# Two projections in tiles of their own, a bias by a product, statistics joined on GpSimd, and three moves in the order of work

## The chip, the cores and the metric

The kernel runs on one core of a Trainium2 chip. A core has a matrix engine (TensorE, called PE in the profile; its weight loads are listed apart as PEld), VectorE (DVE), ScalarE (ACT), GpSimd (POOL) and SyncE (SP), which here only issues DMAs. Each engine runs its own instruction stream in order, and engines wait for one another by semaphores. SP and ACT each have a hardware DMA queue. The metric is the device time of one execution in microseconds, the median of several runs.

## The reference

Input are x and ctx, both (8, 256, 256) in fp32. Two layers are computed, each an attention and a mixture of experts.

1. *Autocorrelation attention.* q = x Wq + bq and k = ctx Wq + bq (256 to 16 columns, the same bias), v = ctx Wq + bq. The circular correlation of q and k over the sequence is averaged over batch and channel, the 12 largest of its 256 lags are taken, and their softmax weighs shifted copies of v. The 16 heads are alike. The result goes through Wout and is added to x.
2. *Balanced assignment.* Scores are layernorm(x) times 8 centroids. Expert 0 takes the 256 tokens with the highest score, expert 1 the best 256 of the rest, and so on. Each expert is 256 to 1024, gelu, 1024 to 256.
3. *Cross attention* of the result with ctx (keys and values from Wkv, 16 heads).
4. *Top-2 mixture of experts* with gated experts and shared ones.

Core of the first two:

```python
q = (Q @ Wq + bq).transpose(0, 2, 1)
k_ = (K @ Wq + bq).transpose(0, 2, 1)
corr = real(ifft(fft(q) * conj(fft(k_)))).mean(axis=(0, 1))
...
for e in range(E):
    s = where(taken, -inf, scores[:, e])
    _, idx = top_k(s, C)
    taken = taken.at[idx].set(True)
```

## The kernel before

The order of the work is written out by hand: the order in which the program names instructions is their order on each engine. PSUM tiles come from pools: `ps_k` with 2 banks, `ps_t` with 4 (tag "pt"), `ps_a` with one bank each for "pqk" and "pg". The program orders all accesses of different engines to one PSUM tile, reads as well as writes.

*Loads (L1296 to L1337).* X and C (the two inputs, in quarters of 512 KB, tiles X and C) and the weights go out on SP's and ACT's queues. Each DMA of these two queues signals one of eight completion counters, given out in turn, and a DMA whose counter is in use waits until the earlier DMA of that counter has landed. The bias bq is needed 8 times over, down the partitions. It goes to DRAM (bqd, L1309) in 8 copies and comes back as a column (bqc, L1320).

*Attention (L1512 to L1790).* PE turns X and C quarter by quarter (`turn`, into XT and CT), while DVE and GpSimd make layernorm's statistics of X. `project` multiplies with Wq: q into half 0 and k into half 1 of the tile pqk (L1445). Rq (row factors of q) is copied out on ACT. ACT then reads k with its bias (L1594) and DVE multiplies q by Rq (L1596). PE makes the Gram product pg (L1674), whose diagonals are summed through a skewed round trip in DRAM (Gd, L1686 and L1694). DVE picks the top lags (L1755 to L1785) and writes them to Wd, and the circulant weights CW come back from there (L1781). In CW's wait PE makes small products into the tile pw: three columns of centroid products, copied by DVE to WCn (L1878), and the search's bounds (pb, L1877), from which DVE makes the steps and offsets of the search (`step`, `off`). Then comes the product with CW (pr, L1906), which DVE scales into R (L1915).

*Rows and statistics (L1918 to L2096).* PE puts x and the attention together, batch by batch ("po"). `take` makes layernorm's statistics of a batch on DVE (two bn_stats and bn_aggr pairs, `tile_stats` L1461 and L1462), copies it out on ACT and stores it to NMd, the table of tokens in DRAM. `act_sums` (L1977 to L1999) does a batch on ACT and GpSimd. `factors` makes the reciprocal standard deviation: eps added (L1471), a power on GpSimd (L1472), one Newton step (L1475 to L1478) in `newton`, and the mean factors (L1481, L1482) in `means`. `widen` (L2013, L2015) and `factor_rows` (L1950) turn factors into rows in one PSUM tile psr; `factors_out` (L2027) copies a half to srow, and `times_factors` (L2024) multiplies the raw scores: n0 for expert 0, SC for the rest. `store_factors` (L1930) puts the factors into NMd, next to their tokens. `attention_columns` (L1360 to L1391) makes, in steps, the norms of the key columns for a bound on the later softmax (`qmax`).

*Searches (L2135 to L2460).* SC goes to SCd in DRAM and row e of it is loaded across all partitions (`load_row`, L2135; SP's queue). `search` (L2158) finds for each expert the threshold that leaves 256 tokens, in rounds: DVE counts (above, L2166), PE sums the counts (pcn, L2183), DVE chooses. `list_tokens` (L2221 to L2291) makes the list of tokens (ob, pid, ids) and gathers them from NMd (R). `ffn` runs the expert on PE (ph L2372, py L2389), DVE adds the bias b2b (Y, L2398), and the rows are scattered to Yd. Each expert's weights are loaded by `load_l0` (L1807, L1809), for experts 0 and 1 ahead of the rows (L1816); the bias b2b is loaded where its expert begins (L2330). All of these are issued by SP, whose DMAs of one queue are worked off by 16 DMA engines, each in its own order.

While PE would wait in this part it works on pieces of the keys and values of the cross attention, 0.43 us each, that lie ready in a list (`work`); `fill(us)` takes as many as the given time holds. FILLS (L2446) sets for each search how much goes ahead of the first count's product, and in each round. After the last expert's search PE is the only limit to the end of the kernel.

Of the kernel before, what the change touches and what calls it, by code (L numbers as in the profile page):

```python
# [19 lines left out]
P = 128  # L20
# [1066 lines left out]
def fast_path(  # L1087
# [195 lines left out]
    bcol = pk.tile([P, 2, NB], F32, name="bcol")  # L1283
    bqd = dram.tile([1, P], F32, name="bqd")
    bkd = dram.tile([1, D], F32, name="bkd")
# [11 lines left out]
    for dst, src, i in (  # L1297
# [9 lines left out]
        nc.sync.dma_start(out=dst[:, i : i + 4, :], in_=src[:, i : i + 4, :])  # L1307

    nc.scalar.dma_start(  # L1309
        out=bqd.rearrange("o (b c) -> (o b) c", b=B),  # L1310
        in_=L0_xattn_bq.partition_broadcast(B),
    )
    nc.scalar.dma_start(
# [5 lines left out]
    nc.scalar.dma_start(out=cen[:, 2, :], in_=L0_ffn_ln_b.partition_broadcast(E))  # L1319
    nc.scalar.dma_start(out=bqc, in_=bqd.rearrange("o (p x) -> p (o x)", x=1))  # L1320
    for src, dst in (
# [34 lines left out]
    bqm = pk.tile([P, NB, 2], F32, name="bqm")  # L1356
    qmax = pk.tile([P, NB], F32, name="qmax")
    kmax = pk.tile([P, NB, NTB], F32, name="kmax")

# [3 lines left out]
    def attention_columns():  # L1363


        for c in range(NB):
            nc.vector.tensor_scalar(
                bqm[:, c, :], mask, bcol[:, 0, c : c + 1], None, ALU.mult
            )
        babs = small.tile([P, NB], F32, tag="babs", name="babs")  # L1370
        nc.vector.scalar_tensor_tensor(
            babs, bcol[:, 0, :], -1.0, bcol[:, 0, :], ALU.mult, ALU.max
        )
        yield

        pn = ps_t.tile([P, NB], F32, tag="pt", name="pn")
        for c in range(NB):
            for kc in range(KC):
                nc.tensor.matmul(
                    pn[:, c : c + 1],  # L1380
                    wsq[:, kc, c * P : (c + 1) * P],
                    ones[:, 0:1],
                    start=(kc == 0),
                    stop=(kc == KC - 1),
                )
            yield
        nc.scalar.activation(qmax, pn, AF.Copy, scale=257.0)
        nc.gpsimd.tensor_tensor(
            qmax, qmax, powers[:, 1:2].to_broadcast([P, NB]), ALU.pow
        )  # L1390
        nc.gpsimd.tensor_tensor(qmax, qmax, babs, ALU.add)  # L1391
        yield

# [42 lines left out]

    pqk = ps_a.tile([P, 2, S], F32, tag="pqk", name="pqk")

    def project(which, weights, src):

        for kc in range(KC):
            for m in range(2):
                for g in range(4):
                    b = 2 * g + m
                    nc.tensor.matmul(  # L1445
                        pqk[32 * g : 32 * g + 32, which, :],
                        weights[:, kc, DH * (1 - m) : DH * (3 - m)],
                        src[:, kc, b * S : (b + 1) * S],
                        start=(m == 0 and kc == 0),
                        stop=(m == 1 and kc == KC - 1),  # L1450
                        skip_group_check=True,
                    )
            yield
# [40 lines left out]
    bsel = pr.tile([P, NCT, 16], F32, name="bsel")  # L1494
    nc.vector.tensor_copy(bsel, fold.to_broadcast([P, NCT, 16]))
    nc.gpsimd.memset(VA[:, :, :, DH:], 0.0)
    nc.gpsimd.memset(VA[:, :, :, DH : DH + 1], 1.0)
# [37 lines left out]
    turn(X, XT, 0, act, act)  # L1535
    turn(C, CT, 0, act, dve)
    pwm = ps_a.tile([P, 3 * DH], F32, tag="pg", name="pwm")
    for kc in range(KC):
# [4 lines left out]
    for kc in range(KC):  # L1543
        nc.vector.memset(WC[:, kc, 0:DH], 0.0)
        nc.vector.memset(WC[:, kc, 2 * DH :], 0.0)
    newton()
    newton = stats_x(4, nc.gpsimd)
# [18 lines left out]
    )  # L1566
    list(project(0, WC, XT))
    turn(C, CT, 12, act, act)
# [10 lines left out]
    nc.vector.memset(cenP, 0.0)  # L1579
    projected = project(1, WZ, CT)  # L1580
    next(projected)
# [11 lines left out]
    list(projected)  # L1593
    nc.scalar.activation(qk[:, 1, :], pqk[:, 1, :], AF.Identity, bias=bqc)  # L1594

    nc.vector.tensor_tensor(qk[:, 0, :], pqk[:, 0, :], Rq, ALU.mult)  # L1596
    nc.gpsimd.tensor_copy(WK, wkv[:, :, :, 0, :])
# [126 lines left out]
    for kc in range(KC):  # L1724
        for g in range(4):
# [7 lines left out]
            )  # L1733
    columns = attention_columns()
    next(columns)
    pb1 = ps_t.tile([P, E * NF], F32, tag="pt", name="pb1")
# [78 lines left out]
    Od = dram.tile([T + P, D], F32, name="Od")  # L1815
    W0 = {e: load_l0(e) for e in range(2)}  # L1816

# [37 lines left out]
    WCn = pa.tile([P, 3, 32], F32, name="WCn")  # L1855
    pw = ps_t.tile([P, 4, 32], F32, tag="pt", name="pw")
    pb = pw[:, 3, 0:E]
# [18 lines left out]
    small_products(2)  # L1876
    nc.tensor.matmul(pb, ones[:E, :], bdiag, start=True, stop=True)  # L1877
    nc.vector.tensor_copy(WCn, pw[:, 0:3, :])  # L1878
    bound = pr.tile([P, E], F32, name="bound")
# [78 lines left out]

    def take(bs):

        for b in bs:
            for h in range(TPB):
                q = TPB * order_b.index(b) + h
                tile_stats(MV[:, q, :], pos[b][:, h, :])
            nc.scalar.copy(rows_of(b), pos[b])
# [60 lines left out]
    def factors_out(m):  # L2026
        nc.scalar.copy(srow[:, m, :], psrs[0][:, m].rearrange("p h t -> p (h t)"))  # L2027
# [5 lines left out]
    squares = act_sums(b[3])  # L2033
    take(b[:1])
    squares()
    take(b[1:2])
    pcp = ps_t.tile([P, 32], F32, tag="pt", name="pcp")
# [6 lines left out]
    spread_rows(*b[6:])  # L2044
    take(b[2:3])
    cP = pa.tile([P, 32], F32, name="cP")
    nc.vector.tensor_tensor(cP, pcp, WCn[:, 2, :], ALU.add)
    newton_a, means_a = factors(0, 8, nc.gpsimd)
    newton_a()

# [17 lines left out]
    take(b[4:6])  # L2068
    next(columns)
    widen(0, 8, nc.scalar)  # L2070
    newton_2, means_2 = factors(8, 12, nc.gpsimd)
    factor_rows(0)
    factor_rows(1)
    rows_part(psx, cP)
    next(columns)
    take(b[6:])
    newton_3, means_3 = factors(12, 16, nc.vector)
    factors_out(0)
    newton_2(nc.vector)
    widen(8, 12, nc.scalar)  # L2080
    factor_rows(2)
    means_a()
    store_factors(0)
    times_factors(n0, ps0, 0)
    newton_3()
    widen(12, 16, nc.vector)
    factor_rows(3)
    times_factors(SC, psx, 0)
    means_2()
    means_3(nc.gpsimd)  # L2090
    store_factors(1)
    factors_out(1)
    nc.scalar.copy(sx1, psx[:, halves[1]])
    times_factors(n0, ps0, 1)
    nc.gpsimd.tensor_tensor(SC[:, halves[1]], sx1, srow[:, 1, :], ALU.mult)
    next(columns)  # L2096

# [44 lines left out]

    nc.sync.dma_start(out=SCd, in_=SC)
    rows = {e: load_row(e) for e in range(1, 3)}
    nc.sync.dma_start(
# [3 lines left out]
    nc.sync.dma_start(out=Od[T:, :], in_=blank[:, 0:D])  # L2149
    rows.update({e: load_row(e) for e in range(3, E - 1)})  # L2150

    def search(e, row, steps, head, each):
# [292 lines left out]

    FILLS = {0: (0.43, [1.29] * 4), 1: (2.15, [1.29] * 4)}  # L2446
    FILLS[2] = FILLS[3] = (2.15, [1.73, 2.58, 1.73, 1.73])
# [1006 lines left out]
```

## Time and profile before

| | us |
|---|---|
| median of 3 runs | 877.67 (877.28 to 878.70) |
| the profiled execution | 878.58 |
| its span | 876.9 |
| PE busy | 854.9 (98%) |
| DVE, ACT, POOL busy | 306.5, 266.1, 213.3 |

Some moments of the profiled execution, in us from the span's start:

| | start |
|---|---|
| first turn of C's third quarter (C8) | 15.99 |
| k from ACT, then q from DVE | 22.94, 23.44 |
| Gram product pg | 23.93 |
| small products out (WCn), R | 39.38, 41.47 |
| last factor rows | 55.57 |
| first count of search 0, first step of search 1 | 57.11, 71.45 |
| Y of the first expert | 95.70 |

A line of the timeline gives the start, the duration, the engine, the line of the kernel, the operation, the output and its inputs, the shapes, and in brackets how long the engine had been idle and who released it. A line of the waits gives the engine and what it was about to do, whom it waited for, and the sum, the number and the longest of such waits. Matmuls are pipelined and their ends are modelled. The profile's span is 1.7 us shorter than the time of the same execution.

### The profile page before, as it was taken

To read this page: it belongs to the slowest core of one execution; us is meant where nothing else is said; L and a number is where in the kernel's file an instruction comes from. 1 tells how busy PE (TensorE), PEld (TensorE's weight loads), DVE (VectorE), ACT (ScalarE), POOL (GpSimd) and SP (SyncE) were. 2 spreads that over 40 slices of the span, in tenths; PEclk is the share of its full clock that TensorE was granted. 3 is DMA by queue.
4 is the path that set the end of the run, shared out by engine and by line. 5 is a ranking of instruction groups with operands and counts; after the bars stand their busy time and mean duration, and the time that the engine had idled before them with its cause. 6 is when DMAs were issued, how large, how long until landed. Compare 5 with 4: busy or idle time off the path is not lost.

```text
span 876.9 us, 11139 instructions
## 1 busy us (share of the span) xinstructions
PE 854.9 (98%) x4178; PEld 533.2 (61%) x4178; DVE 306.5 (35%) x1022; ACT 266.1 (30%) x494; POOL 213.3 (24%) x293
## 2 busy tenths in 40 slices
PE   8999999999999999999999999999999999999997
PEld 7546788788455555545568474747474657474745
DVE  5377876412656765551111212020111111111021
ACT  4344443332677675321110111111111111111110
POOL 7261222302235464423310020201111131111200
PEclk9999999999999999999999999999999999999999
DMA  8385479831610001361111545555657434311130
GB/s 248 132 231 180 158 204 274 277 125 39 167 36 26 1 20 38 122 227 44 68 50 40 177 142 148 163 174 156 181 156 181 150 92 114 85 13 12 18 103 28
DMA packets 87254, 105.22 MB, mean 120 GB/s; under 512 B 8952, under 2 KB 77784, under 8 KB 87160
## 3 DMA queue, kind: packets, MB, share of 16 engines
q1 hardware_dynamic: 78520, 91.10, 33.1%
q0 software_dynamic: 7920, 13.02, 7.1%
q8 instruction: 35, 0.57, 0.3%
q10 hardware_dynamic: 752, 0.30, 0.1%
q14 instruction: 27, 0.22, 0.1%
HBM read 80.61 MB, written 25.37 MB: 121 GB/s over the span
## 4 chain that ended last, share of the span: by engine, by line
PE 87%; DMA 5%; DVE 3%; POOL 2%; ACT 1%; issue 1%; SPq 0%; POOLq 0%; DVEq 0%; ACTq 0%
PE pgt L3074 19%; PE py L3096 19%; PE pu L3074 19%; PE py L2389 5%; PE ph L2372 4%; PE p L2651 4%; PE pv L2666 3%; DMA R<-NMd,ids 3%; PE pp L2717 2%; PE pp L2618 2%; PE pp L1419 2%; PE pp L1398 1%; PE pgu L3269 1%; PE pt L3130 1%; PE pt L1512 1%
## 5 line engine op out<-in xcount | busy, mean ns | idle before, releaser
L3083 DVE TENSOR_TENSOR A<-A,pu 128x512 f32<-128x512 f32 x96 | 66.1, 688 | 364.9 <-PE pu L3074 358.4
L3082 ACT ACTIVATE A<-pgt 128x512 f32<-128x512 f32 x96 | 57.4, 598 | 271.4 <-PE pgt L3074 271.4
L3143 POOL DMA_INDIRECT Od<-Y,ids x32 | 49.7, 1552 | 304.0 <-ACT Y L3156 206.7
L3074 PE MATMUL pgt<-RT,wa 128*128 128x512 f32 x256 | 121.1, 595 | 0.0
L3074 PE MATMUL pu<-RT,wb 128*128 128x512 f32 x256 | 120.3, 592 | 0.0
L3096 PE MATMUL py<-wc,A 128*128 128x256 f32 x512 | 111.8, 379 | 0.0
L3096 PEld LDWEIGHTS py<-wc,A 128*128 128x128 f32 x512 | 96.7, 190 | 13.3 <-issue 0.5
L3074 PEld LDWEIGHTS pu<-RT,wb 128*128 128x128 f32 x256 | 48.6, 190 | 61.2 <-issue 60.0
L2659 ACT ACTIVATE ex<-p,scale 128x512 f32<-128x512 f32 x128 | 77.3, 690 | 27.5 <-PE p L2651 26.2
L3074 PEld LDWEIGHTS pgt<-RT,wa 128*128 128x128 f32 x256 | 47.6, 190 | 54.9 <-issue 54.5
L2372 PE MATMUL ph<-RT,w 128*128 128x256 f32 x256 | 61.7, 389 | 0.8 <-ACT RT L2359 0.7
L2389 PE MATMUL py<-w,A 128*128 128x256 f32 x256 | 61.6, 388 | 0.0
L2372 PEld LDWEIGHTS ph<-RT,w 128*128 128x128 f32 x256 | 45.3, 190 | 8.9 <-ACT A L2381 1.1
L2389 PEld LDWEIGHTS py<-w,A 128*128 128x128 f32 x256 | 46.6, 190 | 6.4
L2891 POOL DMA_INDIRECT Td<-HP,to x32 | 31.7, 991 | 64.5 <-DMA Td<-HP,to 63.8
L2381 ACT ACTIVATE A<-ph,b1c 128x256 f32<-128x256 f32 x64 | 30.1, 473 | 53.9 <-PE ph L2372 49.6
L3074 PE MATMUL pgt<-HT,wa_-1_2734 128*128 128x512 f32 x96 | 45.5, 596 | 0.0
L3074 PE MATMUL pu<-HT,wb_-1_2735 128*128 128x512 f32 x96 | 45.1, 592 | 0.0
L3156 ACT ACTIVATE Y<-py,R 128x256 f32<-128x256 f32 x32 | 15.2, 474 | 96.5 <-PE py L3096 96.5
L2651 PE MATMUL p<-QM,KT 32*128 32x512 f32 x256 | 43.4, 640 | 0.4 <-DVE QM L2632 0.4
L3096 PE MATMUL py<-wc_-1_2736,A 128*128 128x256 f32 x192 | 41.9, 379 | 0.0
L3096 PEld LDWEIGHTS py<-wc_-1_2736,A 128*128 128x128 f32 x192 | 36.4, 190 | 5.8 <-issue 1.0
(445 smaller groups left out, 982.2 us busy)
## 6 DMA issues: line engine op xcount, KB each, us to landing
w<-in_L_ffn_w_dram SPq DMA_DIRECT2D x16, 1024.0 KB
wa<-in_L_ffn_w_e_dram SPq DMA_DIRECT2D x8, 1024.0 KB
wb<-in_L_ffn_w_e_dram SPq DMA_DIRECT2D x8, 1024.0 KB
wc<-in_L_ffn_w_e_dram SPq DMA_DIRECT2D x8, 1024.0 KB
R<-Td SPq DMA_DIRECT2D x8, 530.0 KB
sa<-in_L_ffn_w_e_dram SPq DMA_DIRECT2D x16, 256.0 KB
sb<-in_L_ffn_w_e_dram SPq DMA_DIRECT2D x16, 256.0 KB
sc<-in_L_ffn_w_e_dram SPq DMA_DIRECT2D x16, 256.0 KB
```

The lines of the kernel that those rows point to most:

```text
L2372: nc.tensor.matmul(ph, w1[:, kc, f * P : (f + 1) * P], RT[:, kc, :], start=(kc == 0), stop=(kc == KC - 1),)
L2381: nc.scalar.activation(A[:, f, :], ph, AF.Gelu_apprx_tanh, bias=b1c[:, e, f : f + 1])
L2389: nc.tensor.matmul(py, A[:, f, r * P : (r + 1) * P], w2[:, f, :], start=(f == 0), stop=(f == NF - 1),)
L2651: nc.tensor.matmul(ps[g].rearrange("p m q -> p (m q)"), KT[rows, c, k0 : k0 + P], QM[b][rows, c].rearrange("p m q -> p (m q)"), start=True ...
L2659: nc.scalar.activation(e4[:, g], ps[g], AF.Exp, scale=scale)
L2666: nc.tensor.matmul(pvs[b, c][32 * g : 32 * g + 32, m, :], VA[:, b * TPB + kt, 8 * c + 2 * g + m, :], ex[b, c, kt][:, g, m, :], start=(kt = ...
L2891: nc.gpsimd.indirect_dma_start(out=Td, out_offset=bass.IndirectOffsetOnAxis(ap=to[g][:, k, j : j + 1], axis=0), in_=HP[:, GT * g + j, :], ...
L3074: nc.tensor.matmul(ps, w_[:, kc, fs], xs[kc], start=(kc == 0), stop=(kc == KC - 1),)
L3082: nc.scalar.activation(a, pgt, AF.Silu)
L3083: nc.vector.tensor_tensor(a, a, pu, ALU.mult)
L3096: nc.tensor.matmul(py, A[:, f, s : s + P], wc[:, f, :], start=(f == 0), stop=(f == NF - 1))
L3143: nc.gpsimd.indirect_dma_start(out=Od, out_offset=bass.IndirectOffsetOnAxis(ap=ids, axis=0), in_=Y, in_offset=None, compute_op=ALU.add,)
```

## The change

1. The bias bq is loaded as one column of 16 (`bq16`); both DMAs of the round trip through DRAM go. GpSimd copies a repeated unit matrix (`rep16`), a small product `pbq` spreads the bias over the partitions, and DVE copies it to bqc.
2. q and k get a PSUM tile each: `pq` where pqk was, and `pk_` from the pool of the turned tiles.
3. The products of the column norms leave the stretch of rows and statistics and go into a fifth column block of pw, after pb and ahead of the WCn copy; qmax is made there.
4. For the first three batches DVE only makes the halves' statistics (bn_stats). GpSimd joins the two halves, the variance in six operations ahead of the factors and the mean in two more, after SC. The first Newton step goes to DVE, after all statistics, and the factors' rows are brought into one stretch: factors_out of half 0 now follows the last factor_rows, and all `means` follow SC.
5. The factor stores are issued behind SCd.
6. The second expert's weights are loaded behind the blanks of Yd and Od and the rows 3 to 6.
7. Search 0 takes 0.86 instead of 0.43 us of filler pieces ahead of its first count's product.

```diff
-    bqd = dram.tile([1, P], F32, name="bqd")
+    bq16 = pa.tile([DH, 1], F32, name="bq16")
...
-    nc.scalar.dma_start(
-        out=bqd.rearrange("o (b c) -> (o b) c", b=B),
-        in_=L0_xattn_bq.partition_broadcast(B),
-    )
+    nc.scalar.dma_start(out=bq16, in_=L0_xattn_bq.unsqueeze(1))
...
-    nc.scalar.dma_start(out=bqc, in_=bqd.rearrange("o (p x) -> p (o x)", x=1))
...
-    pqk = ps_a.tile([P, 2, S], F32, tag="pqk", name="pqk")
+    pq = ps_a.tile([P, S], F32, tag="pqk", name="pq")
...
+    rep16 = pa.tile([DH, B, DH], F32, name="rep16")
+    nc.gpsimd.tensor_copy(
+        rep16, ident[:DH, :DH].unsqueeze(1).to_broadcast([DH, B, DH])
+    )
...
+    pbq = ps_k.tile([P, 1], F32, tag="pm", name="pbq")
+    nc.tensor.matmul(
+        pbq,
+        rep16.rearrange("k b c -> k (b c)"),
+        bq16,
+        start=True,
+        stop=True,
+    )
...
+    nc.vector.tensor_copy(bqc, pbq)
...
+    pk_ = ps_t.tile([P, S], F32, tag="pt", name="pk_")
+    projected = project(pk_, WZ, CT)
...
-    nc.scalar.activation(qk[:, 1, :], pqk[:, 1, :], AF.Identity, bias=bqc)
-
-    nc.vector.tensor_tensor(qk[:, 0, :], pqk[:, 0, :], Rq, ALU.mult)
+    nc.scalar.activation(qk[:, 1, :], pk_, AF.Identity, bias=bqc)
+
+    nc.vector.tensor_tensor(qk[:, 0, :], pq, Rq, ALU.mult)
...
-    W0 = {e: load_l0(e) for e in range(2)}
+    W0 = {0: load_l0(0)}
...
-    pw = ps_t.tile([P, 4, 32], F32, tag="pt", name="pw")
+    pw = ps_t.tile([P, 5, 32], F32, tag="pt", name="pw")
...
     nc.tensor.matmul(pb, ones[:E, :], bdiag, start=True, stop=True)
+    column_norms(pw[:, 4, 0:NB])
     nc.vector.tensor_copy(WCn, pw[:, 0:3, :])
...
+    def put_together(q1):
...
+        m = MV[:, 0:q1, 0]
+        nc.gpsimd.tensor_tensor(d, st6[:, :, 1], st6[:, :, 4], ALU.subtract)
+        nc.gpsimd.tensor_tensor(v, st6[:, :, 2], st6[:, :, 5], ALU.add)
+        nc.gpsimd.tensor_tensor(d, d, d, ALU.mult)
+        nc.gpsimd.tensor_scalar(d, d, D / 4.0, None, ALU.mult)
+        nc.gpsimd.tensor_tensor(v, v, d, ALU.add)
+        nc.gpsimd.tensor_scalar(MV[:, 0:q1, 1], v, 1.0 / D, None, ALU.mult)
+
+        def means():
+            nc.gpsimd.tensor_tensor(m, st6[:, :, 1], st6[:, :, 4], ALU.add)
+            nc.gpsimd.tensor_scalar(m, m, 0.5, None, ALU.mult)
...
+                if raw:
+                    nc.vector.bn_stats(st6[:, q, :], pos[b][:, h, :])
+                else:
+                    tile_stats(MV[:, q, :], pos[b][:, h, :])
...
-    take(b[:1])
+    take(b[:1], True)
     squares()
-    take(b[1:2])
+    take(b[1:2], True)
...
-    take(b[2:3])
+    take(b[2:3], True)
...
+    raw_means = put_together(6)
     newton_a, means_a = factors(0, 8, nc.gpsimd)
-    newton_a()
...
     take(b[4:6])
-    next(columns)
+    newton_2, means_2 = factors(8, 12, nc.gpsimd)
+    rows_part(psx, cP)
+    take(b[6:])
+    newton_3, means_3 = factors(12, 16, nc.vector)
+    newton_a(nc.vector)
     widen(0, 8, nc.scalar)
-    newton_2, means_2 = factors(8, 12, nc.gpsimd)
     factor_rows(0)
     factor_rows(1)
-    rows_part(psx, cP)
-    next(columns)
-    take(b[6:])
-    newton_3, means_3 = factors(12, 16, nc.vector)
-    factors_out(0)
     newton_2(nc.vector)
     widen(8, 12, nc.scalar)
     factor_rows(2)
-    means_a()
-    store_factors(0)
-    times_factors(n0, ps0, 0)
     newton_3()
     widen(12, 16, nc.vector)
     factor_rows(3)
+    factors_out(0)
+    times_factors(n0, ps0, 0)
     times_factors(SC, psx, 0)
-    means_2()
-    means_3(nc.gpsimd)
-    store_factors(1)
     factors_out(1)
     nc.scalar.copy(sx1, psx[:, halves[1]])
     times_factors(n0, ps0, 1)
     nc.gpsimd.tensor_tensor(SC[:, halves[1]], sx1, srow[:, 1, :], ALU.mult)
-    next(columns)
+    raw_means()
+    means_a()
+    means_2(nc.gpsimd)
+    means_3(nc.gpsimd)
...
     nc.sync.dma_start(out=SCd, in_=SC)
+    for m in range(2):
+        store_factors(m)
     rows = {e: load_row(e) for e in range(1, 3)}
...
     rows.update({e: load_row(e) for e in range(3, E - 1)})
+    W0[1] = load_l0(1)
...
-    FILLS = {0: (0.43, [1.29] * 4), 1: (2.15, [1.29] * 4)}
+    FILLS = {0: (0.86, [1.29] * 4), 1: (2.15, [1.29] * 4)}
```

## The prediction

> **What bounds the kernel now.** I read the page first, then TensorE's waits, then the stretches where those waits lie. Shares of busy time:
>
> ```profile
> span 876.9 us, 11139 instructions
> PE 854.9 (98%) x4178; PEld 533.2 (61%) x4178; DVE 306.5 (35%) x1022; ACT 266.1 (30%) x494; POOL 213.3 (24%) x293
> ```
>
> PE has 22 us that is not busy. The diff touches nothing that PE works on after the first two experts, so the end moves only by PE's waits in the first 110 us. These, by length:
>
> ```profile
> PE pcn L2183 <- DVE above L2166: 2.5, 2, 1.4
> PE pt L1512 <- DMA X<-in_x_dram: 1.9, 1, 1.9
> ...
> PE pid L2272 <- DVE ob L2268: 1.1, 2, 0.9
> PE pr L1906 <- DMA CW<-Wd: 0.9, 1, 0.9
> PE pg L1674 <- DVE qk L1596: 0.8, 1, 0.8
> ...
> PE pt L1512 <- DMA C<-in_ctx_dram: 0.6, 1, 0.6
> ```
>
> The X wait (to 9.84) and the pg wait (to 23.93) are what parts of this change can shorten; pr, pcn and pid are where it can lengthen. Why X is late shows in SP's waits, and in the windows (columns: stretch, length, busy us of PE, PEld, DVE, ACT, POOL, PE's clock, DMA share, GB/s):
>
> ```profile
> SPq L1307 <- DMA bqd<-in_L_xattn_bq_dram: 3.2, 1, 3.2
> ...
> SPq L1307 <- DMA WZ<-in_L_xattn_Wq_dram: 0.7, 1, 0.7
> ```
> ```profile
> 5.50:8.00 2.50, 2.49 (x24) 2.36 (x22) 2.33 (x11) 2.49 (x5) 0.90 (x2) 1.00 0.73 150
> 8.00:9.00 1.00, 0.00 (x0) 0.00 (x0) 0.96 (x4) 0.40 (x1) 0.76 (x2) 1.00 1.02 242
> 12.00:15.00 3.00, 3.00 (x16) 2.81 (x15) 1.99 (x8) 1.80 (x4) 2.01 (x6) 0.50 1.09 349
> ```
>
> X4 is not issued until bqd has landed, and in that gap the memory moves 150 GB/s where it later moves 349.
>
> **1. Loads (bqd and bqc gone).** The two hardware queues' DMAs take eight completion counters in turn, so the ninth waits for the first. Landings before: bqd 4.99, X4 9.70 (issued 5.00), C4 11.33, X8 12.85, X12 14.35, C8 15.85, C12 17.36: 1.5 us per 512 KB once the stream runs. With bqd's second DMA gone X4 is the eighth and waits for nobody; C4 waits for the small bq16 and is issued at about 5.0 or before. X4 then follows C0 (landed 6.44) by one transfer: about 8.0, C4 9.5, and the last, C12, 15.5 instead of 17.36: **-1.85**. PE follows its loads here (C8 landed 15.85, its turn starts 15.99; C12 17.36, then 18.85 after the q projection). Upper end -2.3, if the 0.50 clock of 11.9 to 15.3 also goes; lower end 0, if X4 lands no earlier. I take the transfer arithmetic. The added product pbq costs one small matmul (0.28 us, the small products pc at 22.80), and stands at 7.5 to 8.3, where PE has nothing (0.00 busy in 8 to 9). Without that cover: +0.28. The rep16 copy on GpSimd (about 0.4 us) goes ahead of VA's memset, which nothing needs before 30 us.
>
> *A rule beside this row.* PE's clock was granted 0.50 for 3.41 us, after 3.4 us in which PE was busy 43% but never idle throughout. The Trainium skill, "TensorE: Matmul & The Clock Gate", Part 1 (the HAM clock gate), has the halving follow an idle window of some 3.4 us; no whole idle window stands ahead of this one. By the page the change has no such window either and the clock stays up; by the row a stretch as thin as 43% would halve it again and cost about 1 us of part 1.
>
> **2. q and k apart.** Both lie in one PSUM tile, and q's product waits for k's ACT read:
>
> ```profile
> 22.94 0.47 ACT L1594 ACTIVATE qk<-pqk,bqc 128x256 f32<-128x256 f32 x1 [0.66 <-PE pqk L1445]
> 23.44 0.42 DVE L1596 TENSOR_TENSOR qk<-pqk,Rq 128x256 f32<-128x256 f32 x1 [2.74 <-ACT qk L1594]
> ```
>
> Apart, DVE may go when Rq is there (22.28), and k's 22.94 + 0.47 is last: pg starts about 23.47 instead of 23.93: **-0.46**. It can't be more while k stays last; 0 if the new bank (k takes one of the transposes' four) delays k's projection by as much. Front: -2.3, ends -2.8 and -0.46 (or 0 with both bad).
>
> **3. Column norms.** Before, their four products stand at 51.54 and 54.13, where PE waits for nobody afterwards and fillers can't be pushed later than they are: taking them away gives 0 to -0.3; I take 0, since DVE and POOL set that stretch. Their new place is behind pb, ahead of the WCn copy, in the same bank:
>
> ```profile
> 39.38 0.26 DVE L1878 COPY WCn<-pw 128x96 f32<-128x96 f32 x1 [3.33 <-PE pw L1877]
> ...
> 41.47 0.48 DVE L1915 TENSOR_SCALAR R<-pr,rtot 128x256 f32<-128x256 f32 x1 [0.71 <-PE pr L1906]
> ```
>
> 2 x 0.61 = 1.22 us of PE (the rows at 51.54 and 54.13), then ACT's qmax read (0.19): WCn starts near 40.85. From WCn to the last `off` takes 1.38 (39.38 to 40.76), so DVE comes to R at about 42.2 where 41.47 was needed: **+0.7**. Ends +0.2 (only PE's 1.22 over its 0.94 wait for CW) and +0.9.
>
> **4. Statistics.** Six BATCH_NORM_AGGREGATE of 0.18 leave DVE; each shortens its pair by 0.13 (0.53 against 0.40). But GpSimd's new joining is six ops at about 0.27, 1.65, behind its op at 47.90, so the variances are there at 49.75 rather than 48.96; the power (1.67) ends 51.75 against 50.92, and two more behind it 54.1. newton_a's four steps (0.8) move from POOL to DVE. The last factor rows' product comes at about 55.25, before 55.57: **-0.3**. Then the order: rows are copied out half by half, and half 0 now waits until the last product into that bank is done, so two more reads of 0.43 lie ahead of search 0:
>
> ```profile
> 55.57 0.63 PE L1950 MATMUL psr<-ident,sexp 128*32 128x128 f32 x8 [0.28 <-DVE sexp L2015]
> ...
> 56.25 0.37 ACT L2027 COPY srow<-psr 128x256 f32<-128x256 f32 x1 [1.69 <-PE psr L1950]
> ...
> 56.65 0.42 DVE L2024 TENSOR_TENSOR n<-ps,srow 128x256 f32<-128x256 f32 x1 [0.83 <-ACT srow L2027]
> ```
>
> **+0.87** there. With part 3 search 0 starts 0.7 - 0.3 + 0.9 = 1.3 later than before, on before's clock (ends -0.3, +1.9).
>
> **5. Factor stores behind SCd.** Search 1 was not ready-bound but row-bound:
>
> ```profile
> 71.45 0.75 DVE L2158 SCALAR_TENSOR_TENSOR n<-n,lo,row 128x512 f32<-128x512 f32 x1 [1.53 <-DMA row<-SCd]
> ```
>
> DVE was ready at 69.92 and row 1 landed at 71.33. SP's row load (issued 65.02) waited 3.6 us for the factor stores, issued before SCd. Now SCd is issued at about 59.15, eight GpSimd ops give the means at 61.3, and the stores are issued from 60.2 to 62.05. Issue to landing of such stores was 2.8, 4.3, 5.9 (least, median, most): the first, by the median, lands at 64.5, the last, by the least, at 64.85, against 63.8 to 64.9 before. The row load goes then, and lands 6.3 later as it did (65.02 to 71.33): about 71.2. DVE is ready at 69.92 + 1.27 = 71.2. So the 1.3 of parts 3 and 4 is swallowed by the row's wait, and search 1 starts about where it did: **-0.1** (71.35). Ends: -0.4; +2.9, if the last store takes 5.9 (67.95 + 6.3 = 74.3).
>
> **6. One more filler piece (0.43) ahead of search 0's first count.** It lies in a pcn wait of 1.1: 0 to -0.46, I take **-0.2**; an excess would only add 0.1.
>
> **7. Second expert's weights.** 2 MB, before landed at 49 to 52 us, now queued on SP behind rows 3 to 6. Those rows keep four DMA engines busy till 91:
>
> ```profile
> 86.00:90.00 4.00, 4.00 (x33) 2.88 (x32) 3.21 (x15) 2.21 (x5) 0.00 (x0) 1.00 0.26 101
> ```
>
> Row 6 landed at 91.21, and the bias b2b(0) behind it at 91.54, for DVE's Y:
>
> ```profile
> 95.70 0.42 DVE L2398 TENSOR_TENSOR Y<-py,b2b 128x256 f32<-128x256 f32 x1
> ```
>
> The weights' share on those four engines, 16 packets of 4 KB at 0.159 and 64 of 1 KB at 0.046, is 5.5 us, so b2b, queued behind, lands at about 96.9 instead of 91.5. Y wants it at 95.4 to 95.7: DVE stands about 1.3 us, with a search's steps queued behind, and PE's wait for pid (at 99.4) grows by that: **+1.3**, ends 0 (the rows end earlier, or b2b overtakes) and +2.0. The weights themselves are wanted at 101.2, 5 us later than they land. Moving them away from 49 to 52 gives nothing I can name: that stretch waits on DVE and POOL.
>
> *Sum:* -1.85 - 0.46 - 0.1 - 0.2 + 1.3 = -1.3. The profiled execution (878.58, span 876.9 and 1.7 around it) lies 0.9 above the median of the runs shown; the sum goes on both alike: 877.3 there, 876.4 as a median.
>
> **Rivals.** 0.2% is 1.75 us here: 875.9 and 879.4 are the edges.
> A. The sum as above, 876.4 (own range 875.4 to 877.4).
> B. b2b lands in time: without part 7, 877.67 - 2.6 = 875.0. For it: the weights' DMAs may spread over engines that rows leave free; against: four engines at 0.26 share carry the rows, and b2b needs every one of its own.
> C. The loads don't come earlier, by a counter I mapped wrongly or the half clock again: only -0.46 - 0.2 + 1.0 = +0.3, 878.0. For it: 0.50 came without idle time; against: the 150 GB/s hole has a named wait.
> D. Slower: the stores, started behind SCd, land 5.9 after issue (their longest before), row 1 at 74.3 and search 1 with it: -2.3 + 2.9 + 1.3 + about 0.2 = +2.1, 879.8. It decides once row 1 lands later than 74.0 on before's clock. For it: the stores wait for GpSimd's eight ops and POOL's products for SC; against: the median is 4.3 with the weights' 2 MB in the way, which have gone.
>
> **How the numbers follow.** A 0.35, B 0.29, C 0.14, D 0.22. A's lower third is below 875.9, so faster 0.29 + 0.11 = 0.40; same 0.24 + 0.14 = 0.38; slower 0.22. The range: from 0.6 below B, 874.3, to D's centre 879.8, which leaves out some 2 in 10.
>
> **What would show it.** X4 lands by 8.2 and C12 by 15.7; PE's X wait under 0.5; q before k's end; R at 42.0 to 42.4 less the front's gain; psr copies back to back ahead of search 0; row 1 ending DVE's wait at about 69 on the new clock; b2b ending a DVE wait at Y. I am wrong if the row wait grows by over 2 us, if X4 still ends past 9, or if search 0 starts before 55.

## The result

The changed kernel takes 882.75 us (median; 882.1 to 883.75), the kernel before 877.85 (877.28 to 878.7). The ratio is 1.0056, with a 95% interval of 1.0039 to 1.0073: slower by 4.9 us. Forecast were 876.4, and 874.3 to 879.8 as the range.

The page of the changed kernel's profile, first lines:

```profile
span 880.5 us, 11146 instructions
PE 858.2 (97%) x4180; PEld 535.3 (61%) x4180; DVE 309.7 (35%) x1021; ACT 266.2 (30%) x494; POOL 213.6 (24%) x298
```

PE is 3.3 us busier with almost the same products: its clock was 0.50 for 10.24 us (97.93 to 108.17), in before's trace for 3.41. PE's waits in the first 135 us, changed kernel:

```profile
PE ppl L2288 <- DVE before L2276: 3.3, 1, 3.3
PE psr L1958 <- ACT sexp L2045: 1.8, 1, 1.8
PE pcn L2215 <- DVE above L2198: 1.8, 2, 1.3
...
PE pt L1509 <- DMA X<-in_x_dram: 0.4, 1, 0.4
...
PE pg L1682 <- ACT qk L1602: 0.4, 1, 0.4
```

The waits that were to shrink did so: X from 1.9 to 0.4, pg from 0.8 to 0.4. The wait for the factor rows (psr) grew from 0.7 in two pieces to 1.8. One of 3.3 is new, for DVE in the third expert's list. DVE's own timeline there:

```profile
94.32 0.16 DVE L2205 TENSOR_TENSOR w<-lo,off 128x1 f32<-128x1 f32 x1
98.09 0.42 DVE L2430 TENSOR_TENSOR Y<-py,b2b 128x256 f32<-128x256 f32 x1 [3.61 <-DMA b2b<-in_L_ffn_b_dram]
```

DVE stood 3.61 us for the first expert's bias, with the list's steps queued behind. In the same stretch the granted clock falls (windows of the changed kernel; columns as in the prediction):

```profile
96.00:98.00 2.00, 0.00 (x0) 0.00 (x0) 0.00 (x0) 1.09 (x2) 0.00 (x0) 0.98 0.36 135
98.00:103.00 5.00, 4.27 (x29) 3.28 (x28) 4.46 (x22) 0.00 (x0) 1.25 (x2) 0.50 0.16 60
103.00:108.00 5.00, 4.34 (x13) 2.64 (x12) 2.67 (x14) 1.98 (x4) 0.74 (x1) 0.50 0.91 285
```

Where the two traces stand to one another, at moments found on DVE's timeline:

| | before | changed | difference |
|---|---|---|---|
| Gram product pg (PE) | 23.93 | 22.22 | -1.71 |
| small products out (WCn) | 39.38 | 38.86 | -0.52 |
| R | 41.47 | 40.34 | -1.13 |
| cP | 48.34 | 46.65 | -1.69 |
| search 0, first count | 57.11 | 56.52 | -0.59 |
| search 1, first step | 71.45 | 69.80 | -1.65 |
| search 3, first step | 91.83 | 90.53 | -1.30 |
| Y of the first expert | 95.70 | 98.09 | +2.39 |
| search 4, first step | 104.61 | 109.38 | +4.77 |
| end of the span | 876.9 | 880.5 | +3.6 |

The front's gain is there and stays until search 3. Between search 3 and search 4 the changed kernel loses 6.1 us: 3.61 is DVE's wait, 2.4 more lie between Y and search 4 (8.91 us in before, 11.29 here). By the end of this trace 1.2 of it has come back.

### The profile page after: what moved, and what is told of

The parts are those of the page before. It is cut to its first block, busy times and chain, and to the rows that moved or that the text cites. A ratio compares the mean times of both kernels' runs of the same rounds, so it can differ in the third digit from the quotient of the medians.

```text
span 880.5 us, 11146 instructions
## 1 busy us (share of the span) xinstructions
PE 858.2 (97%) x4180; PEld 535.3 (61%) x4180; DVE 309.7 (35%) x1021; ACT 266.2 (30%) x494; POOL 213.6 (24%) x298
## 4 chain that ended last, share of the span: by engine, by line
PE 88%; DMA 3%; DVE 3%; SPq 2%; POOL 2%; ACT 1%; issue 1%; POOLq 0%; ACTq 0%; DVEq 0%
PE pgt L3106 19%; PE py L3128 19%; PE pu L3106 19%; PE py L2421 6%; PE ph L2404 5%; PE p L2683 4%; PE pv L2698 3%; DMA b2b<-in_L_ffn_b_dram 2%; PE pp L2749 2%; PE pp L2650 2%; DMA R<-NMd,ids 2%; PE pp L1391 1%; PE pgu L3301 1%; SPq L2164 1%; PE pt L3162 1%; SPq L2180 1%
```

## Experiments

All ratios are to runs of the kernel before on the same chip in the same series; differences in us are the ratio's times 878. Parts are numbered as in the prediction: 6 is the filler piece, 7 the late weights. Times of landing are the last completion of a DMA in the trace.

**The weights back at their old place.**

```diff
-    W0 = {0: load_l0(0)}
+    W0 = {e: load_l0(e) for e in range(2)}
...
-    W0[1] = load_l0(1)
```

> The changed kernel with the second expert's weights back at their old place (part 7 undone, all else kept). Theory Q (the first expert's bias is queued behind those weights, lands at 98.0, and DVE, then PE, stand): from search 3 to search 4 the changed kernel loses 6.1 us (-1.3 to +4.8 against before), so about 882.7 - 6.1 = 876.6 (875.8 to 877.4), DVE's wait at the first Y gone and no granted clock of 0.50 between 98 and 108. Rival M (the new order of rows and statistics costs the time, the stall only shows it): 880 or more.

Measured: 879.41 against 879.53, ratio 0.9987 (0.9971 to 1.0003), -1.1 us. DVE no longer waits at the first Y:

```profile
97.39 0.42 DVE L2429 TENSOR_TENSOR Y<-py,b2b 128x256 f32<-128x256 f32 x1
```

The absolute number misses the expectation since this chip's kernel before is slower too; against before it is where theory Q had it (876.6 against 877.85 is -1.2), and rival M's 880 against 877.85 would be +2.1 or more. The profiled execution did have a clock of 0.50 near 103 to 106 and in three other places; the section on the hardware comes back to this.

**The bias ahead of the late weights.**

```diff
+    b2b0 = pr.tile([P, D], F32, name="b2b0")
+    nc.sync.dma_start(out=b2b0, in_=L0_ffn_b2[0].partition_broadcast(P))
     W0[1] = load_l0(1)
...
+        if e == 0:
+            b2b = b2b0
+        else:
             b2b = pf.tile([P, D], F32, tag="b2b", name="b2b")
             nc.sync.dma_start(out=b2b, in_=L0_ffn_b2[e].partition_broadcast(P))
```

> The changed kernel with the weights as late as it has them, but the first expert's bias loaded ahead of them on the same queue. Theory Q: the weights themselves are in time (wanted at about 100, landed 94.0 and 97.7), only the bias was not: 876.6 (875.8 to 877.4). Rival W (the late weights themselves are waited for, or their transfer slows the second expert's gather): 879 or more, with a wait of PE for w or of ACT for R.

Measured: ratio 1.0008 (0.9994 to 1.0022), +0.7 us. The first Y on DVE's timeline:

```profile
94.57 0.42 DVE L2435 TENSOR_TENSOR Y<-py,b2b 128x256 f32<-128x256 f32 x1
```

No wait, with the weights as late as in the changed kernel. About 4 of the 4.9 us are gone by moving one small DMA, and in the trace PE has no wait for w. So the bias behind the weights is the larger part: Q. The result lies between the two forecasts, though, and its interval reaches both; it is 1.8 us above the run with the weights early, with intervals that overlap. Five of its twelve runs had a mean clock of 0.991 or 0.992, of the twelve with the weights early one (0.990). Why is not shown, and a smaller cost of the late weights themselves is not excluded.

**The bias between the weights.** The second weight tile is loaded in two halves, the bias between them.

```diff
+    nc.sync.dma_start(out=w2_1[:, 0:4, :], in_=w2s[:, 0:4, :])
+    nc.sync.dma_start(out=b2b0, in_=L0_ffn_b2[0].partition_broadcast(P))
+    nc.sync.dma_start(out=w2_1[:, 4:, :], in_=w2s[:, 4:, :])
```

> The changed kernel with the bias ahead of the last half megabyte of the late weights: it should land near 96 instead of 98.0, wanted at 94.4. This sets the length of the stall. If the clock halves only after an idle time of PE as long as the 3.3 us seen, then here PE idles some 1.5 us, the clock stays at 1.00 and the time is 876.6 plus about 1.0 to 1.5, near 877.8 (877.0 to 878.6). If any stall of PE halves the clock: 880 or more. If the stall alone and no clock is the cost: 882.7 - 2 = 880.7.

Measured: ratio 1.0020 (1.0004 to 1.0036), +1.8 us. DVE's wait was 2.61 and not 1.5, because the row loads in this execution were issued at 64.24, 1.4 later than in the changed kernel's trace. PE stood idle for 2.3 us at a stretch and the clock halved nonetheless, from 100.1 to 110.4. So the idle time need not be 3.3 us for that, and the run does not tell stall from clock.

**PE kept busy in the stall**, with the products one list earlier at first.

```diff
+        if e == 1:
+            pd = ps_h.tile([P, CAP], F32, tag="ph", name="pd")
+            for _ in range(11):
+                nc.tensor.matmul(
+                    pd, ones, low[0][0][:, 0:CAP], start=True, stop=True
+                )
         ppl = ps_t.tile([P, NT], F32, tag="pt", name="ppl")
```

> The changed kernel with eleven products of 256 columns (about 0.28 us each, 3.1 us in all, written to a bank that nobody reads) put on PE ahead of the second list's prefix product, where PE stood idle for 3.3 us. The stall stays as long as it was. Theory C (the idle time halves the granted clock for the next 10.3 us, and this is the larger part of the loss): clock 1.00 throughout, time down by 3.0 to 4.4, 878.3 to 879.7. Rival S (DVE's stall is the whole cost, the clock runs beside it): unchanged within 0.5, 882.2 to 883.2.

Measured: ratio 1.0047 (1.0030 to 1.0064), +4.1 us. Here the products came at 85.1, ahead of the second list, and took 4.91 us, not 3.1; DVE waited 4.2 us for that list's ppl, and by the time Y came (100.97) the bias was there. It says nothing on the clock, but it prices the place: a delay of 4.2 us for both engines between search 2 and search 3 costs most of its length (+4.1, where the run with the bias ahead, which has no stall either, has +0.7).

With `e == 2` they stand in the stall:

> The changed kernel with the eleven products of 3.1 us on PE ahead of the third list's prefix product (the one that stood idle for 3.3 us; the run before this had put them one list too early, where they delayed the first expert's products). Theory C: the stall stays, the clock does not halve behind it, and the time falls by about two of the three stretches, 2 x 1.7 = 3.4 (2.4 to 4.4) under the changed kernel of this chip. Rival S (the stall alone costs): within 0.7 of it.

Measured: ratio 1.0045 (1.0027 to 1.0063), +4.0 us; the changed kernel measured beside it (next) has 1.0055. The windows and the first Y:

```profile
98.00:103.00 5.00, 4.42 (x39) 3.64 (x37) 4.27 (x22) 0.43 (x1) 1.01 (x1) 1.00 0.25 83
103.00:108.00 5.00, 4.34 (x16) 2.85 (x15) 2.83 (x14) 2.29 (x5) 0.98 (x1) 0.67 0.86 278
```
```profile
98.42 0.42 DVE L2436 TENSOR_TENSOR Y<-py,b2b 128x256 f32<-128x256 f32 x1 [3.95 <-DMA b2b<-in_L_ffn_b_dram]
```

The stall is as long as before (3.95), the clock is 1.00 behind it until one halved stretch later, and the time falls by 0.9 us, inside the intervals. I had expected 2.4 to 4.4. (The products took 4.91 us again, to 99.9, but DVE's next step of the list, `place`, came 2.14 after Y as in before.) So the stall is the larger cost, and the halved clock's share is not clear of zero. Two of these runs had a mean clock of 1.000 and took 880.07 and 880.33; the nine of before with 0.999 or more took 875.5 to 876.8: the stall costs some 4 us without any halved clock. The traces agree: from Y to search 4 it takes 8.90 to 8.91 us in the four without a halved stretch there, 10.4 to 10.5 in those with one (this run 10.49), and 11.0 to 11.8 in the three with three (the changed kernel 11.29). The first halved stretch costs 1.6 there, two more only 0.5 to 1.3; why they cost less is not shown.

**The changed kernel again**, measured beside that run.

> The changed kernel once more, as the measure for the others on this chip, and for how much of its time is clock. In the trace its clock was 0.50 for 10.3 us (98 to 108), which is three stretches of 3.41 us and takes 5.1 us of full-clock work; before had one such stretch. Theory C: nearly every run has a mean clock of 0.994 or less (5.1 of 880). Then 882 to 885. If the halving were chance, runs with 0.998 should be seen among them at 879 or less.

Measured: 883.41, ratio 1.0055 (1.0035 to 1.0075). Five of six runs had a mean clock of 0.993, one 0.997 (881.19). The three halved stretches are the rule in this kernel (the four runs above had 0.993 or 0.994 too), but even the run without most of them is 3.2 above before's median.

**The late weights alone, on the kernel before.**

```diff
-    W0 = {e: load_l0(e) for e in range(2)}
+    W0 = {0: load_l0(0)}
...
     rows.update({e: load_row(e) for e in range(3, E - 1)})
+    W0[1] = load_l0(1)
```

> The kernel before with the late second weights alone (part 7 on its own). Theory Q: the bias lands at about 98 here too, Y wanted it at 95.7, so a stall of 2 to 3 us, and a halved clock behind it where it is long enough: 4 to 6.5 above before. Rival M (the order of rows and statistics carries the loss): within 1.0 of before.

Measured: ratio 1.0001 (0.9987 to 1.0015). A clear miss: theory Q as I had put it falls. Late weights alone cost nothing that can be told from zero. The first Y, and SP's issues of the row loads and the bias:

```profile
94.55 0.42 DVE L2399 TENSOR_TENSOR Y<-py,b2b 128x256 f32<-128x256 f32 x1
```
```profile
60.77 1.27 SPq L2135 DMA_DIRECT2D row<-SCd  x2
...
69.29 6.51 SPq L2135 DMA_DIRECT2D row<-SCd  x4
...
79.61 7.57 SPq L2331 DMA_DIRECT2D b2b<-in_L_ffn_b_dram  x1
```

The row loads go out at 60.77, where the kernel before had 65.02 and the changed kernel this:

```profile
62.80 1.26 SPq L2164 DMA_DIRECT2D row<-SCd  x2
...
71.47 6.28 SPq L2164 DMA_DIRECT2D row<-SCd  x4
...
81.48 8.39 SPq L2362 DMA_DIRECT2D b2b<-in_L_ffn_b_dram  x1
```

Without the weights' 2 MB ahead of them the old kernel's factor stores land 4.4 us sooner (the last at 60.1, against 64.5), the rows follow at once, and row 6, the weights and the bias (landed at 94.46) with them: just in time. In the changed kernel all had run 1.7 us ahead by then, and yet the row loads came 2.0 later. What held them (SP's waits, 55 to 110 us, changed kernel):

```profile
SPq L2164 <- DMA NMd<-rm: 1.9, 1, 1.9
```

The factor stores: their means were moved to the end on GpSimd and the stores themselves behind SCd. The row loads need nothing of them, but by the program the rows' tiles come from a pool opened after the one with rm has closed, so they can lie in its memory and wait until rm has been read. (The next run moves rm's pool and the order of issue together, so the memory alone is not tested.) That makes theory I: the bias is late by *late rows plus late weights* in one queue. Neither alone does it: with the weights early the row loads went at 65.02 and the bias had landed at 91.20, six us ahead of Y.

**Rows ahead of the stores, in the changed kernel.**

```diff
-    rm = pa.tile([P, NT, 2], F32, name="rm")
+    rm = pr.tile([P, NT, 2], F32, name="rm")
...
-    for m in range(2):
-        store_factors(m)
     rows = {e: load_row(e) for e in range(1, 3)}
+    for m in range(2):
+        store_factors(m)
```

> The changed kernel with the tile of the factors (rm) kept in a pool that stays open, and the factor stores issued behind the row loads 1 and 2 instead of ahead of them. In the changed kernel the row loads were issued at 62.8 to 63.1, 0.2 after the last factor store had landed, because the rows' tiles lie in the memory of the pool that holds rm. Theory I (the late bias is the sum of late rows and late weights: rows 3 to 6, the weights and the bias are one queue, so a row load that starts sooner brings the bias sooner): row 1 issued near 59.8, so all behind it 3 us sooner; bias near 95.1 instead of 98.0 to 98.7, the stall 0.5 to 1 instead of 3.6 to 4.1; 3.0 to 4.0 under the changed kernel, that is 1.5 to 3.0 above before. Rival W2 (the bias lands late because of the weights' own 2 MB, wherever the rows start): within 1.0 of the changed kernel, 4.5 or more above before.

Measured: ratio 1.0015 (0.9999 to 1.0030), +1.3 us. SP's issue of rows 1 and 2, and the first Y:

```profile
59.58 1.26 SPq L2164 DMA_DIRECT2D row<-SCd  x2
```
```profile
96.07 0.42 DVE L2430 TENSOR_TENSOR Y<-py,b2b 128x256 f32<-128x256 f32 x1 [0.63 <-DMA b2b<-in_L_ffn_b_dram]
```

The row loads go 3.2 us sooner, the bias wait falls from 3.6 to 0.63, and 3.6 of 4.9 us are gone with the weights still late. The interplay is shown, not W2. (The stores now land at 68.5 to 69.5 and the first expert's gather about 2 us later, so search 3 starts 1 us later; this gives some of it back.)

**New front alone, and with the late weights.** Parts 1 and 2 of the diff on the kernel before; then parts 1, 2 and 7; then these with the stores behind the rows.

> The kernel before with parts 1 and 2 alone (the bias by a product; q and k in tiles of their own). The Gram product came 1.71 earlier in the changed kernel's trace. Theory Q: this gain reaches the end whole, 1.7 (1.0 to 2.4) under before. Rival F: a later wait (row 1's landing, the lists, the gathers) takes it back: within 0.6 of before.

Measured: ratio 0.9983 (0.9968 to 0.9998), -1.5 us. By the median the front's gain is carried to the end; the weak end of the interval, -0.2, does not exclude rival F.

> The kernel before with parts 1, 2 and 7 (new front and late weights, the old middle). With the late weights alone the bias landed at 94.46 and the first Y took it at 94.55, so there is no margin. Theory I: in the old middle the row loads go early (60.8, here 1.7 sooner), the bias lands near 92.9 where Y wants it at 92.9, no stall: 1 to 2 under before. Rival W2: the bias late by 1.7 or more, 0.5 or more above before.

Measured: ratio 0.9984 (0.9973 to 0.9995), -1.4 us. The row loads go at 59.34; the first Y:

```profile
93.26 0.42 DVE L2409 TENSOR_TENSOR Y<-py,b2b 128x256 f32<-128x256 f32 x1 [0.50 <-DMA b2b<-in_L_ffn_b_dram]
```

Late weights with the old middle: a wait of 0.50 where the new middle has 3.61.

> The same (parts 1, 2 and 7 on the kernel before), with rm in the open pool and the factor stores behind the row loads 1 and 2, so that the rows wait for the scores alone. If the old middle's stores hold the rows back by 2 us or so, search 1 and the queue behind it start sooner and the bias has a margin of 1 to 2 us: 1.3 to 2.5 under before, and not above the run with the stores ahead. If search 1 does not wait for row 1 any more, the two are alike within 0.5.

Measured: ratio 1.0028 (1.0009 to 1.0047), +2.5 us, a miss of 4 us. SP's queue and the first Y:

```profile
58.69 1.26 SPq L2143 DMA_DIRECT2D row<-SCd  x2
60.00 5.30 SPq L1940 DMA_DIRECT2D NMd<-rm  x4
65.34 1.78 SPq L2155 DMA_DIRECT2D Yd<-blank  x1
67.16 2.49 SPq L2159 DMA_DIRECT2D Od<-blank  x1
69.70 6.20 SPq L2143 DMA_DIRECT2D row<-SCd  x4
```
```profile
96.60 0.42 DVE L2409 TENSOR_TENSOR Y<-py,b2b 128x256 f32<-128x256 f32 x1 [1.83 <-DMA b2b<-in_L_ffn_b_dram]
```

Rows 1 and 2 gain only 0.65 (the stores of the old middle did not hold them long), but the stores behind them took 5.30 us to issue instead of 2.91, rows 3 to 6 went 1.7 later than in the run before (68.03), and the table that the first expert gathers from was complete at 69.1 instead of 58.3, its rows there at 79.1 instead of 76.1. In an ordered queue what is put ahead is paid by what comes behind.

**The middle: parts 3 to 6 alone**, then its two halves.

> The kernel before with parts 3 to 6 alone (column norms moved, statistics joined on GpSimd, factor stores behind the scores', one more piece), without the new front and with the second weights at their old place. By the traces search 0 starts 1.1 later than the Gram product's gain would have it, and search 1 is where it was. Theory I: -0.3 to +1.0 against before, since the bias lands in time with the weights in their old place. Rival M: the middle by itself costs 3 or more.

Measured: ratio 1.0019 (1.0008 to 1.0030), +1.7 us, above what I expected. In its trace search 0 starts 2.0 later than in before, search 1 1.0 and the first Y 1.4. But 0.9 of the 2.0 is there at cP already, in an execution with a halved stretch near 41.

> The kernel before with part 3 alone (column norms ahead of the WCn copy). In the changed kernel's trace R came 0.57 later than the front's gain would have it, and the scores' small product cP had all of it back. Theory S (the middle's 1.7 us come from the order of the statistics and factor rows): within 0.7 of before. Rival N (they come from the norms' 1.2 us ahead of WCn): 1.0 to 2.0 above before.

Measured: ratio 0.9996 (0.9981 to 1.0010), -0.4 us. R comes 0.53 later and search 0 0.26 later. No cost that can be told from nothing, and not 1.0 to 2.0.

> The kernel before with parts 4 to 6 alone (statistics joined on GpSimd, one stretch of factor rows, stores behind the scores', one more piece), the column norms where they were. Theory S: search 0 starts 1 to 2 us later and search 1 by 1, as in the run of parts 3 to 6; 1.0 to 2.2 above before. Rival N: within 0.7 of before.

Measured: ratio 1.0008 (0.9993 to 1.0023), +0.7 us. Search 0 starts 0.65 later than in before, and 1.1 later counted from cP. The half-way result leaves the rest of the middle's 1.7 open: the two halves add to +0.3 with intervals of 1.3 either way.

**The bias ahead, in the good combination** (parts 1, 2 and 7 on the kernel before, and the bias ahead of the late weights, as in the second experiment).

> The kernel before with parts 1, 2 and 7, and the first expert's bias ahead of the late weights. With the weights ahead DVE waited 0.5 us for the bias; this takes the wait away, so 0.3 to 0.5 under that run, 1.5 to 2.2 under before. If the late bias cost nothing in that place, it is no lower than 1.4 under before.

Measured: 877.19 against 880.28, ratio 0.9970 (0.9955 to 0.9984), -2.6 us. DVE has no wait at the first Y. This kernel is faster than before and than the changed one. That it is better than the run without the bias ahead is not shown: the intervals overlap.

Runs that differ in that queue, side by side:

| kernel | rows 1 and 2 issued | row 3 to row 6 landed | first Y | DVE's wait for the bias | ratio to before |
|---|---|---|---|---|---|
| before | 65.02 | 7.68 | 95.70 | none | 1 |
| late weights alone | 60.77 | 9.61 | 94.55 | none | 1.0001 |
| front, late weights | 59.34 | 10.20 | 93.26 | 0.50 | 0.9984 |
| front, late weights, bias ahead | 59.50 | 10.39 | 92.42 | none | 0.9970 |
| changed, rows first | 59.58 | 10.73 | 96.07 | 0.63 | 1.0015 |
| front, late weights, rows first | 58.69 | 11.02 | 96.60 | 1.83 | 1.0028 |
| changed, bias between | 64.24 | 10.91 | 98.37 | 2.61 | 1.0020 |
| changed | 62.80 | 10.56 | 98.09 | 3.61 | 1.0056 |
| changed, bias ahead | 63.31 | 10.29 | 94.57 | none | 1.0008 |
| changed, weights early | 65.02 | 7.73 | 97.39 | none | 0.9987 |

The third column is a cost that I had not seen: wherever the late weights stand behind the rows in the queue, the rows themselves land more slowly.

## Why the prediction was wrong

**Parts 1 and 2: right, somewhat smaller.** X4 was issued without waiting and the loads came 1.59 sooner instead of 1.85 (the turns of C8 and C12: 15.99 to 14.40, 18.85 to 17.26). A wait that I had left out, PE's 0.26 for rexp from GpSimd, took some of it: the next product, pR, is 1.25 sooner. q and k apart brought exactly the 0.46 forecast (1.71 - 1.25). Their timeline in the changed kernel:

```profile
21.07 0.42 DVE L1604 TENSOR_TENSOR qk<-pq,Rq 128x256 f32<-128x256 f32 x1 [0.95 <-ACT Rq L1600]
...
21.69 0.47 ACT L1602 ACTIVATE qk<-pk__438,bqc 128x256 f32<-128x256 f32 x1 [0.66 <-PE pk__438 L1438]
```

DVE is ahead of ACT now, and k is last. In sum -1.71 against -2.31; as runs, -1.5 us alone. The half clock at 11.74 to 15.15 in before was not there in this trace.

**Parts 3 to 6: the sizes on the path were near, the claim that a wait swallows them was not safe.** R was +0.58 against +0.7, all given back by cP; search 0 started 1.1 later than the front would have had it, against 1.27; search 1 at +0.06 (-1.65 against -1.71), where -0.1 was forecast. But row 1 did not end DVE's wait, as it should have: it had landed at 68.70, search 1 began at 69.80. And when the stores land was priced by a misreading: the 2.8, 4.3 and 5.9 us belong to the gathers from NMd, not to stores. The factor stores took 6.9 to 8.8 us in before and 2.0 to 2.9 in the changed kernel; that the last landed at 62.59, where the forecast less the front's gain has 62.55, is luck. Run alone, the middle costs 1.7 us. In that trace search 1 starts 1.0 later, and the row wait takes up only part of search 0's 2.0; how much of either is the halved stretch ahead of them is open. Part 6 has no run of its own.

**Part 7: DVE waits for the bias as forecast, but the term is mis-sized, 3.61 instead of 1.3, and this is the step that failed.** On before's clock the forecast had the bias at 96.9 and wanted at 95.4 to 95.7. The front's 2.3 moves both: 94.6 and about 93.3. In the trace the head of the queue kept to that. The row loads went at 62.80, 2.2 sooner than in before, and row 3 landed at 80.86, 2.7 sooner. Row 6 landed at 91.42, no sooner than in before (91.21). The step that failed is that rows 3 to 6 would keep before's pace ("keep four DMA engines busy till 91"), and that the weights would cost only what follows row 6. The weights move while the rows still do:

```profile
86.00:90.00 4.00, 4.00 (x35) 2.97 (x34) 2.81 (x14) 2.61 (x6) 0.00 (x0) 1.00 1.08 235
```

Here the changed kernel moves 235 GB/s where before moved 101 (the prediction's row for the same stretch), and with the weights early it is 101 again:

```profile
86.00:90.00 4.00, 4.00 (x35) 3.12 (x35) 3.75 (x17) 2.61 (x6) 0.00 (x0) 1.00 0.26 101
```

From row 3 to row 6 it took 10.56 us instead of 7.68, and the median packet of 2 KB, which is what the rows are made of, 125 ns instead of 84. In all six traced kernels with early weights it is 7.7 to 8.0 us and 84 ns, in all eleven with late ones 9.6 to 11.0 and 113 to 134; the two pairs that differ in nothing else (before and late weights alone, changed and weights early) show it too. How the transfers hinder one another no run shows. So row 6 came 2.5 later than 88.9, its forecast place, and the bias 6.58 behind row 6 instead of 5.7: 98.0, 3.4 later than 94.6. Y was wanted at 94.48, 1.2 later than 93.3, as the front brought 1.71 instead of 2.31 and 1.3 of that was left at search 3. 1.3 + 3.4 - 1.2 = 3.5 is the 3.61 of the trace.

The stores' hold on the rows was in the forecast. It is no less a cause, since without it the stall falls to 0.63 (rows ahead of the stores). The middle kept the queue 2.0 later than the late weights alone have it, so that the front's gain became stall here: the parts do not add up singly.

**What I left out** is what the stall does to the clock: three stretches at 0.50 behind it, where the sum had none. By the busy-wait run their share of the loss is about 0.9 us and not clear of zero; by the traces, 2.4 from Y to search 4 against none in before, of which the first stretch has 1.6 and comes in runs without the stall too. How much of the 4.9 is clock stays open between the two.

**The rivals.** B had the bias in time; it erred to the other side of A than the runs did. D had a slower end (879.8) from row 1 landing after 74.0; row 1 landed at 68.70. The slower end came by another road, through the far end of the queue, and went beyond D.

## What to carry to other kernels

A queue that is worked off in order is a chain like any engine's: when something large is put into it, list everything behind it with the time at which each is wanted, and put the small early ones ahead. Price not only what waits behind it but also what is still moving ahead of it: here the loads in front took up to 3.3 us longer. Size a transfer's slack on the new schedule, consumer and producer each by its own releaser; a gain ahead of the consumer that does not reach the producer is slack lost. And look at what a load waits for: here it was a store whose data it does not need.

## What the runs showed of the hardware

The time of one and the same kernel varies with the granted clock. Among 25 runs of the kernel before in one series, the nine with a mean clock of 0.999 or more took 875.5 to 876.8 us (median 876.2), the thirteen with 0.995 or less 877.9 to 880.6 (878.6). In the traces the clock is either 1.00 or 0.50, in stretches of 3.41 us or a multiple, at places that change from run to run: before had one at 11.74 to 15.15; the run with the weights early had five stretches, near 39, 56 to 62 (two), 104 and 165, and this profiled execution took 884.47 where its fastest took 876.84. A difference of 2 us between two single executions of this kernel says nothing.

The Trainium skill, "TensorE: Matmul & The Clock Gate", Part 1 (The HAM clock gate), has a free-running window of 3413 ns, the half clock after an idle window and the full one after a busy window. The length agrees, and so does the run-to-run phase. But the window ahead need not be idle throughout: PE was busy in 0.25 of it in the changed kernel, in 0.33 with the bias between (no idle time above 2.3 us), in 0.39 in before. Nor does any busy window bring the full clock back: in the changed kernel the three halved ones had PE busy in 0.77, 0.81 and 1.00, and only the third ended it. Cut along these windows, the 17 traces show more: after 0.44 or less the clock always halved, between 0.46 and 0.64 sometimes, at 0.65 or more never, but for three windows near 35 to 39 us with a busy PE, which stay unexplained. A halved clock went on after windows with 0.62 to 0.89 and ended after 0.89 to 1.00.

That the bias could not pass the weights agrees with "DMA: Bandwidth & Descriptors", Queues, rings and completion order, by which each DMA engine takes a ring's descriptors in order: in the changed kernel the last weights landed at 97.65 and the bias at 98.00, and DVE waited 3.61 us; with the bias ahead it landed at 92.28, and DVE did not wait.
